# Two adaLN layers on one core: the second layer's modulation moved into the end of the latent attention

## The chip, the cores and the metric

The kernel runs on one core of a Trainium2 chip. The metric is the device time of one execution in microseconds (us); smaller is better. A core has five engines with a queue each: TensorE (PE in the profile; its weight loads are PEld), VectorE (DVE), ScalarE (ACT), GpSimd (POOL) and SyncE (SP), which here issues nearly all DMAs. They run beside each other and wait for each other through semaphores.

## The reference, cut to what matters

```python
mod = (silu(c0) @ wmod0).reshape(1, 6, 256)          # sa, ca, ga, sb, cb, gb of layer 0
ga, gb = (2*(g >= 0) - 1) * maximum(abs(g), 0.25)     # for both gates
h = layernorm(x) * (1 + ca) + sa
x = x + ga * attn0(h)     # gates[0] * latent attention + gates[1] * 16 small heads of 16
h = layernorm(x) * (1 + cb) + sb
x = x + gb * ffn0(h)      # 8 experts, dense
mod = (silu(c1) @ wmod1).reshape(1, 6, 256)          # the same six of layer 1, from c1 alone
h = layernorm(x) * (1 + ca) + sa
x = x + ga * attn1(h)     # 16 causal heads of 16 with ALiBi
h = layernorm(x) * (1 + cb) + sb
x = x + gb * ffn1(h)      # 2 shared and 16 routed experts
```

x is 1024 tokens by 256, float32; c0 and c1 are single rows of 256, so each layer's modulation is one row of 1536 numbers. Layer 1's row doesn't depend on x and isn't read before layer 1's input. The latent attention of layer 0 has 16 heads: scores of 128 + 64 features, of which 64 are turned by rotary angles, and values that come from a latent of 64 features.

## The kernel before, in words

Tokens lie in two halves of 512 (index `i`), each of four tiles of 128. Products go to PSUM: two tiles `sc` of 1024 columns, and four of 512 that are named `nn` and `mm` in turn (`mm_tile`). A float32 product stands in the profile as two MATMUL records, called passes here. The stages, in order:

1. **Start.** x arrives; 18 products of the identity with itself (L751) run on PE while nothing else can; `first_modulation` (L104) makes shift and scale of layer 0's first input out of one third of wmod0, in 8 products with one column each; `by_feature` (L213) transposes the normalised half 0; four `products` (L520) with wA follow, then half 1.
2. **The small heads of layer 0.** A first part takes 128 by 1024 scores per item (L317) and their maxima on DVE (L323). 11 such items are made ahead, and a generator `fill` (L792) puts other products between them, three parts per item: projections, `latents_by_token` (L571), `fold_weights` (L584, products L590 and L606) and last `modulation` (L115) with the five remaining thirds of both layers. For each third `rows` (L122) multiplies the repeated silu(c) with 512 columns of wmod (L126, 4 passes) and copies the result out; `rest_of` (L132) transposes parts of one row of it by products with a one (L139, one column) and forms the gates on DVE (L141 to L159). A second part, in steps, recomputes scores (L351) beside the remaining first items and multiplies with v (L383).
3. **The latent attention** (L888 on): 16 units (head pair p, half i) of 8 tiles each. `scores` (L685, maximum L689, exponential L868) runs two tiles ahead, `transposed` (L876) turns the probabilities, and a table `beside` says what else goes with which tile: in the tiles n+9 to n+12 `over_latents` multiplies a unit's probabilities with the latents in four parts of 64 products (L907, 128 passes each), after `by_latent` (L890) has transposed one over the sums, which ACT copies out as `bc` (L894); `out_part` (L925) multiplies with the folded weights. In units with i = 0 the next pair's query and key parts (L653, L668, L669) go to the tiles n+5 to n+9; `turned` (L618) has ACT scale and swap them (L628, L632) and POOL add the rotary terms (L635 to L639).
4. **The drain.** After tile 127 the last unit's four parts, `by_latent`, the transposes of half 0 (L221) and the last `out_part` are all that is left. DVE meanwhile adds half 0's residual and normalises it.
5. The experts of layer 0, then all of layer 1.

PE's order is written by hand in all stages. That of ACT, DVE and POOL is by hand up to the end of `fill`; later a planner orders them, as it does SP's. A change in `beside` thus moves ACT's and DVE's order too.

```python
def over_tiles(n, parts):
    for k in range(3):
        at(n + k, lambda: next(parts, None))
```

Of the kernel before, what the change touches and what calls it, by code (L numbers as in the profile page):

```python
# [8 lines left out]
F32 = mybir.dt.float32  # L9
# [5 lines left out]
P = 128  # L15
T = 1024
# [26 lines left out]
def adaln_two_layers(ctx: ExitStack, tc: tile.TileContext, a: dict, out: bass.AP):  # L43
# [33 lines left out]

    def modulation_third(wp, l, i):
        w = wp.tile([P, 2, 512], F32, tag="wm", name="wm")
        cols = slice(i * 512, (i + 1) * 512)  # L80
        nc.sync.dma_start(w, a[f"wmod{l}"].rearrange("(k p) m -> p k m", p=P)[:, :, cols])
        return w

# [10 lines left out]

    cs = base.tile([P, 4], F32, name="cs")
    one = base.tile([1, 1], F32, name="one")
    modT, gates_bc, by_token = {}, {}, {}
# [5 lines left out]
    def first_modulation(w):  # L103

        pm = mm_tile()
        for j in range(4):
            for k in range(2):
                nc.tensor.matmul(
                    pm[:, j : j + 1], w[:, k, j * P : (j + 1) * P], cs[:, k : k + 1], start=(k == 0), stop=(k == 1)
                )  # L110
        nc.vector.tensor_copy(modT[0][:, 0:2], pm[:, 0:2])
        nc.vector.tensor_scalar_add(modT[0][:, 2:4], pm[:, 2:4], 1.0)

    def modulation(wp, crep):


        thirds = [(0, 1), (0, 2), (1, 0), (1, 1), (1, 2)]
        wm = [modulation_third(wp, *at) for at in thirds[:3]]
        ms = {}
        yield  # L120

        def rows(n):  # L122
            l, i = thirds[n]
            ps = mm_tile()
            for k in range(2):
                nc.tensor.matmul(ps, crep[:, 2 * l + k, :], wm[n][:, k, :], start=(k == 0), stop=(k == 1))  # L126
            ms[n] = wp.tile([P, 512], F32, name="m", bufs=2)
            evacuate(ms[n], ps)
            if n + 3 < len(thirds):
                wm.append(modulation_third(wp, *thirds[n + 3]))  # L130

        def rest_of(n):  # L132
            l, i = thirds[n]
            m = ms.pop(n)
            mt = modT[l]
            pm = mm_tile()
            for j in ((0, 1, 2, 3), (6, 7), (8, 9))[i]:
# [356 lines left out]
    with pool("l0a") as l0, pool("mla") as ml:  # L494
# [198 lines left out]
        with pool("pat") as pat:  # L693
# [11 lines left out]
            with pool("absorb") as ab:  # L705
# [8 lines left out]
                with pool("first") as fp:  # L714
                    first = modulation_third(fp, 0, 0)
                    nc.sync.dma_start(wA, a["wA"].rearrange("(k p) m -> p k m", p=P))
# [31 lines left out]
                    nc.scalar.activation(cs, cT, AF.Silu)  # L748
                    ps = mm_tile()
                    for _ in range(18):  # L750
                        nc.tensor.matmul(ps[:, :P], ident, ident, start=True, stop=True)  # L751
                    norms = [normalized(i) for i in range(2)]
# [4 lines left out]
                    whole(norms[0])  # L757
                    first_modulation(first)
                    by_feature(0, 0, 0)
                    next(norms[1])  # L760
# [31 lines left out]
                def fill():  # L792
                    crep = ab.tile([P, 4, P], F32, name="crep")
                    nc.vector.tensor_copy(crep, cs.unsqueeze(2).to_broadcast([P, 4, P]))
                    with pool("wmod", 3) as wp:
                        mods = modulation(wp, crep)
                        next(mods)
                        for i in range(2):
                            project(qT, put_q, wt[1], 1, i)
                            yield  # L800
                        for t in range(NT):
                            project_v(v, wt[2], t)
                            if t % 2:
                                yield
                        yield from latents_by_token(ab)
                        yield from fold_weights(qn, wkv, wo)
                        yield from mods

# [38 lines left out]
        with pool("mla1") as m1, pool("mla2", 2) as m2:  # L847
# [47 lines left out]

            def over_latents(u, part):


                n = T // 32 // 4
                if part == 0:  # L900
                    avs[u] = [mm_tile() for _ in range(4)]
                pt, av = pts[u], avs[u]
                for b in range(n * part, n * part + n):
                    for r in range(4):
                        row = slice(32 * r, 32 * r + 32)
                        for j in range(2):
                            nc.tensor.matmul(  # L907
                                av[r][64 * j : 64 * j + 64, :P], kv32[row, b, :], pt[j][row, b, :],
                                start=(b == 0), stop=(b == 4 * n - 1),
                            )  # L910
                if part < 3:
                    return
                del pts[u], avs[u]
                cxs[u] = m2.tile([P, 4, P], F32, name="cx")
                bc = bcs.pop(u)
                for r in range(4):
                    q = slice(32 * r, 32 * r + 32)
                    nc.vector.tensor_mul(
                        cxs[u][:, :, q], av[r][:, :P].rearrange("p (t q) -> p t q", t=4), bc[:, :, q]
                    )  # L920
# [16 lines left out]

            def over_tiles(n, parts):

                for k in range(3):  # L940
                    at(n + k, lambda: next(parts, None))

            for u, (p, i) in enumerate(units):
                n = 8 * u
                if u + 1 < len(units):
                    at(n + 8, by_latent, u)
                for part in range(4):
                    at(n + 9 + part, over_latents, u, part)
                    if u + 1 == len(units) and part == 1:

                        at(n + 9 + part, by_latent, u, lambda: sc_tile()[:, :512])
                for t, m in enumerate((14, 15, 16, 16)):
                    at(n + m, out_part, u, t)
                if p + 1 < NH // 2:
                    if i == 0:
                        at(n, weights_of, p + 1)
                    over_tiles(n + 5, query_part(p + 1, i, True))
                    over_tiles(n + 6, query_part(p + 1, i, False))
                    if i == 0:
                        over_tiles(n + 6, key_part(p + 1, 0))  # L960
                        over_tiles(n + 7, key_part(p + 1, 1))
            def reload():
                for i in range(2):
                    nc.sync.dma_start(x[i], xv[:, 4 * i : 4 * i + 4, :])

            over_tiles(1, query_part(0, 1, True))
            over_tiles(3, query_part(0, 1, False))
            at(4, latents_of_odd)
            at(112, reload)
            last = 8 * len(units)  # L970
            at(last, residual, 0, gates_bc[0][:, :HID])
            at(last, lambda: whole(normalized(0)))
            at(last + 5, by_feature, 0, 1, 0, True)
            with tc.manual_schedule(engines={mybir.EngineType.PE}):
# [513 lines left out]
```

## Time and profile before

| what | us |
|---|---|
| median of 3 runs (all: 1382.57, 1378.88, 1382.86) | 1382.57 |
| the profiled execution, its own time | 1383.18 |
| its span, first to last instruction | 1381.4 |
| PE busy (share of the span) | 1322.2 (96%) |
| DVE busy | 810.2 (59%) |
| ACT busy | 605.2 (44%) |
| POOL busy | 206.7 (15%) |

The table's busy times come from the page's first part. PE is the engine with work nearly always; what counts are the places where it waits and the stretches where its clock is granted at half. Times in the text are microseconds from the span's start. In lines of the timeline the first number is the start, the second the length of the group; in brackets stands how long the engine idled before it, and what ended that. In a table of windows each engine has its busy time and the instructions that touch the window; then come the granted TensorE clock, the share of the DMA engines and GB/s.

### The profile page before, as it was taken

What the parts mean: (1) busy time and instruction counts of PE and PEld (TensorE: products, weight loads), DVE (VectorE), ACT (ScalarE), POOL (GpSimd) and SP (SyncE); (2) the same over time, 40 slices, a digit from 0 to 9 for tenths busy, and PEclk for the clock granted to TensorE, in tenths of its full rate; (3) what the DMA queues carried; (4) which work ended last, traced back from release to release, by engine and by line L of the source; (5) the groups of instructions that cost most, each with busy time, mean ns of one, the idle gap of its engine ahead of it and who ended that gap; (6) DMA issues with size and microseconds to landing.
All of it is one profiled execution on the core that took longest, in us unless ns stands there. A gap on an engine that the chain in (4) does not pass through costs nothing. (4 is left out here: it accounts for less than half of the span.)

```text
span 1381.4 us, 33034 instructions
## 1 busy us (share of the span) xinstructions
PE 1322.2 (96%) x14664; PEld 724.9 (52%) x14664; DVE 810.2 (59%) x1243; ACT 605.2 (44%) x1083; POOL 206.7 (15%) x194
## 2 busy tenths in 40 slices
PE   9999999988999999999999889999999998999998
PEld 6542323324555555555555565565556444566665
DVE  3677777735676776767676765443465766143222
ACT  4436665644655645454655322211034644511111
POOL 2000000041424334141424001000000031010000
PEclk9999999999999999999999999999999999999999
DMA  9210000000000000000001203222210000234441
GB/s 260 76 32 1 1 1 1 1 1 16 6 6 9 6 6 6 7 7 6 2 3 36 74 4 82 69 84 70 69 56 25 2 2 1 85 96 147 152 154 56
DMA packets 56600, 59.33 MB, mean 43 GB/s; under 512 B 15047, under 2 KB 42184, under 8 KB 56458
## 3 DMA queue, kind: packets, MB, share of 16 engines
q1 hardware_dynamic: 55914, 57.22, 13.8%
q8 instruction: 115, 1.88, 0.6%
q14 instruction: 27, 0.22, 0.1%
q10 hardware_dynamic: 544, 0.00, 0.0%
HBM read 55.05 MB, written 1.12 MB: 41 GB/s over the span
## 5 line engine op out<-in xcount | busy, mean ns | idle before, releaser
L323 DVE TENSOR_REDUCE mx<-sc 128x2 f32<-128x1024 f32 (+3 forms) x224 | 240.0, 1106 | 45.5 <-PE sc L317 17.3
L868 ACT ACTIVATE pr<-sc,nmax 128x1024 f32<-128x1024 f32 x128 | 142.6, 1114 | 218.8 <-DVE nmax L689 212.7
L876 DVE STREAM_TRANSPOSE pt<-pr 128x1024 f32<-128x1024 f32 x128 | 158.9, 1242 | 122.4 <-ACT pr L868 122.4
L317 PE MATMUL sc<-kT,qT 32*128 32x512 f32 (+3 forms) x896 | 211.0, 594 | 19.7 <-DVE mx L323 19.3
L351 PE MATMUL mm<-q,kT 32*128 32x512 f32 (+3 forms) x388 | 195.8, 606 | 4.5 <-DVE t L626 3.0
L351 PE MATMUL nn<-q,kT 32*128 32x512 f32 (+3 forms) x388 | 195.1, 604 | 0.5 <-DVE qf L675 0.5
L689 DVE TENSOR_REDUCE nmax<-sc 128x1 f32<-128x1024 f32 x128 | 153.9, 1203 | 16.8 <-PE sc L685 13.4
L907 PE MATMUL mm<-pt,kv 32*64 32x128 f32 x4096 | 135.2, 274 | 8.0 <-ACT bc L894 5.4
L907 PE MATMUL nn<-pt,kv 32*64 32x128 f32 x4096 | 135.4, 274 | 3.2 <-issue 1.7
L361 ACT ACTIVATE pt<-mm 128x512 f32<-128x512 f32 (+2 forms) x194 | 107.9, 556 | 60.5 <-PE nn L351 34.0
L907 PEld LDWEIGHTS mm<-pt,kv 32*64 32x64 f32 x4096 | 117.3, 130 | 32.0 <-issue 24.8
L907 PEld LDWEIGHTS nn<-pt,kv 32*64 32x64 f32 x4096 | 116.9, 130 | 28.7 <-issue 22.2
L361 ACT ACTIVATE pt<-nn 128x512 f32<-128x512 f32 (+2 forms) x194 | 107.9, 556 | 53.0 <-PE mm L351 21.4
L317 PEld LDWEIGHTS sc<-kT,qT 32*128 32x128 f32 x896 | 66.9, 186 | 116.0 <-DVE mx L323 95.8
L685 PE MATMUL sc<-kf,qf 128*128 128x512 f32 x256 | 125.7, 614 | 1.1 <-ACT pr L868 1.1
L685 PE MATMUL sc<-x,qf 128*128 128x512 f32 x256 | 123.3, 606 | 1.4 <-ACT pr L868 1.4
L635 POOL TENSOR_TENSOR t<-t,cos 128x512 f32<-128x512 f32 x32 | 41.1, 1286 | 527.4 <-ACT sw L632 268.1
L1242 DVE TENSOR_TENSOR he<-he,row 128x512 f32<-128x512 f32 x46 | 31.7, 692 | 132.9 <-ACT he L1234 107.3
L1234 ACT ACTIVATE he<-sc,b 128x512 f32<-128x512 f32 x43 | 29.6, 688 | 123.7 <-PE sc L1233 123.7
L1233 PE MATMUL sc<-hT,w 128*128 128x512 f32 x172 | 80.7, 593 | 0.0
L632 ACT COPY sw<-t 32x512 f32<-32x512 f32 x116 | 71.6, 617 | 2.0
L685 PEld LDWEIGHTS sc<-x,qf 128*128 128x128 f32 x256 | 45.5, 189 | 50.5 <-issue 46.4
(362 smaller groups left out, 2009.8 us busy)
## 6 DMA issues: line engine op xcount, KB each, us to landing
w<-in_moe_w_dram SPq DMA_DIRECT2D x50, 256.0 KB
w<-in_wg_dram SPq DMA_DIRECT2D x16, 256.0 KB
w<-in_wu_dram SPq DMA_DIRECT2D x16, 256.0 KB
w<-in_wd_dram SPq DMA_DIRECT2D x16, 256.0 KB
row<-gD SPq DMA_DIRECT2D x14, 256.0 KB
wm<-in_wmod_dram SPq DMA_DIRECT2D x6, 512.0 KB
x<-in_x_dram SPq DMA_DIRECT2D x4, 512.0 KB
wo<-in_o_dram SPq DMA_DIRECT2D x1, 2048.0 KB
```

The source lines that it names most:

```text
L317: nc.tensor.matmul(sc[:, i, :n], qT[r, g, qt * P : (qt + 1) * P], kT[r, g, c * 512 : c * 512 + n], start=True, stop=not diag,)
L323: nc.vector.tensor_reduce(mx[:, qi, c, 2 * pair : 2 * pair + 2], sc[:, :, :n], AX.X, ALU.max)
L351: nc.tensor.matmul(ps[:, q0:], kT[r, g, kc * P : (kc + 1) * P], state[u]["q2"][r, q0:], start=True, stop=not diag,)
L361: nc.scalar.activation(pt[:, 2 * pair + i, q0:], ps[:, q0:], AF.Exp)
L632: copy(sw[32 * (s ^ 1) : 32 * (s ^ 1) + 32, :], t1[32 * s : 32 * s + 32, :])
L635: nc.gpsimd.tensor_mul(t1, t1, cos[:, cols])
L685: nc.tensor.matmul(sc[:, c], qfs[p, i][j][:, t * P : (t + 1) * P], kf[p % 2][j][:, c], start=True, stop=True)
L689: nc.vector.tensor_reduce(nmax, sc, AX.X, ALU.max, negate=True)
L868: nc.scalar.activation(pr, sc, AF.Exp, bias=nmax, accum_out=sums[u][:, t, j : j + 1])
L876: nc.vector.transpose(pts[u][j][:, :, 32 * t : 32 * t + 32], prs.pop(n).rearrange("p (b k) -> p b k", k=32))
L907: nc.tensor.matmul(av[r][64 * j : 64 * j + 64, :P], kv32[row, b, :], pt[j][row, b, :], start=(b == 0), stop=(b == 4 * n - 1),)
L1233: nc.tensor.matmul(ps, w1[:, k, :], hT[i][:, k, :], start=(k == 0), stop=(k == 1))
```

## The change

- `modulation_third` loads each third into two tiles of 128 by 512 with a DMA each, instead of one tile of 128 by 2 by 512.
- Six more identity products run on PE between `first_modulation` and the first `by_feature`.
- `fill` keeps only layer 0's two thirds, and puts them ahead of `fold_weights`. Both rows are copied out by ACT now (they alternated).
- Layer 1's three thirds go to the drain: their loads are asked for in tile 116, into the buffers of the key and query parts (`sw`, `t1`); the first `rows` goes ahead of the last unit's part 0, and after each of the parts 0, 1 and 2 come the next `rows` and a `rest_of`. They use `sc` tiles.
- Of the next pair's key parts the product and first copy go one tile forward (n+5 and n+6 instead of n+6 and n+7); their second and third piece stay in their tiles. The query part that isn't turned now follows both keys' products in n+6.
- `by_feature` of half 0 is listed one tile earlier; on PE it stands after the last part, as before.

In the compiled order, 12 passes of L126 and 16 of L139 leave the stretch before the steps and stand in the drain. On DVE, layer 1's 14 gate instructions follow half 0's normalisation.

```diff
-    def modulation_third(wp, l, i):
-        w = wp.tile([P, 2, 512], F32, tag="wm", name="wm")
+    def modulation_third(l, i, tiles):
         cols = slice(i * 512, (i + 1) * 512)
-        nc.sync.dma_start(w, a[f"wmod{l}"].rearrange("(k p) m -> p k m", p=P)[:, :, cols])
-        return w
+        for k, w in enumerate(tiles):
+            nc.sync.dma_start(w, a[f"wmod{l}"][k * P : (k + 1) * P, cols])
+        return tiles
...
-        thirds = [(0, 1), (0, 2), (1, 0), (1, 1), (1, 2)]
-        wm = [modulation_third(wp, *at) for at in thirds[:3]]
+        wm = [modulation_third(*at, tiles()) for at in thirds]
...
-            ms[n] = wp.tile([P, 512], F32, name="m", bufs=2)
-            evacuate(ms[n], ps)
-            if n + 3 < len(thirds):
-                wm.append(modulation_third(wp, *thirds[n + 3]))
+            ms[n] = m_tile()
+            nc.scalar.copy(ms[n], ps)
...
                     first_modulation(first)
+                    nothing(6)
                     by_feature(0, 0, 0)
...
                         yield from latents_by_token(ab)
+                        yield from mods
                         yield from fold_weights(qn, wkv, wo)
-                        yield from mods
...
+            def over_tiles(tiles, parts):
+                for n in tiles:
+                    at(n, lambda: next(parts, None))
...
+                    for part in range(4):
+                        at(n + 9 + part, over_latents, u, part, 4)
+                        if part == 1:
+                            at(n + 9 + part, by_latent, u, lambda: sc_tile()[:, :512])
+                        for _ in range(2):
+                            at(n + 9 + part, lambda: next(mods, None))
...
-                    over_tiles(n + 5, query_part(p + 1, i, True))
-                    over_tiles(n + 6, query_part(p + 1, i, False))
+                    over_tiles((n + 5, n + 6, n + 7), query_part(p + 1, i, True))
                     if i == 0:
-                        over_tiles(n + 6, key_part(p + 1, 0))
-                        over_tiles(n + 7, key_part(p + 1, 1))
+                        over_tiles((n + 5, n + 7, n + 8), key_part(p + 1, 0))
+                        over_tiles((n + 6, n + 8, n + 9), key_part(p + 1, 1))
+                    over_tiles((n + 6,), query_part(p + 1, i, False))
...
+            mods = modulation(
+                [(1, i) for i in range(3)], lambda: [m2.tile([P, 512], F32, tag=t, name=t, bufs=3) for t in ("sw", "t1")],
+                lambda: m2.tile([P, 512], F32, name="m", bufs=2), lambda: sc_tile()[:, :512],
+            )
+            at(116, lambda: next(mods))
             last = 8 * len(units)
+            at(last, lambda: next(mods))
             at(last, residual, 0, gates_bc[0][:, :HID])
             at(last, lambda: whole(normalized(0)))
-            at(last + 5, by_feature, 0, 1, 0, True)
+            at(last + 4, by_feature, 0, 1, 0, True)
```

## The prediction, made before the change was run

> **What bounds the kernel now.** First the page: PE is busy for 96% of the span, so a gain must come from PE's waits, from half clock, or from work that moves into such waits. Next the table of windows, cut where the granted clock changes:
>
> ```profile
> 3.34:6.75 3.41, 3.41 (x18) 3.41 (x18) 1.15 (x5) 0.00 (x0) 2.40 (x5) 1.00 0.90 277
> 6.75:10.16 3.41, 2.85 (x26) 2.69 (x25) 3.09 (x13) 0.21 (x1) 1.03 (x1) 1.00 1.10 348
> 10.16:13.58 3.42, 2.77 (x14) 2.37 (x13) 1.80 (x9) 0.94 (x2) 0.95 (x1) 0.50 1.03 325
> 13.58:16.99 3.41, 3.41 (x8) 2.69 (x9) 0.49 (x2) 1.31 (x5) 0.29 (x2) 0.50 1.17 300
> ...
> 88.67:92.09 3.42, 1.85 (x11) 0.70 (x6) 3.32 (x10) 0.00 (x0) 0.00 (x0) 1.00 0.00 0
> 92.09:95.50 3.41, 3.41 (x11) 2.35 (x13) 2.58 (x3) 2.34 (x5) 0.00 (x0) 0.50 0.00 0
> ```
>
> See the clock column: it falls to half at 10.16 and at 92.09, each time for 6.83 us, on a grid of 3.41 us. Ahead of 92.09 PE was busy for 1.85 us of 3.42; ahead of 10.16 it was mostly on products of one column. Then PE's and DVE's timeline where the small heads' steps begin:
>
> ```profile
> 87.05 0.70 PE L317 MATMUL sc<-kT,qT 32*128 32x512 f32 x2 [0.55 <-DVE mx L323]
> 90.94 0.66 PE L351 MATMUL mm<-q,kT 32*128 32x512 f32 x1 [1.57 <-DVE modT L144]
> ```
> ```profile
> 85.77 2.36 DVE L323 TENSOR_REDUCE mx<-sc 128x2 f32<-128x1024 f32 x2 [0.38 <-PE sc L317]
> 88.50 1.22 DVE L323 TENSOR_REDUCE mx<-sc 128x2 f32<-128x1024 f32 x1
> 92.23 2.58 DVE L323 TENSOR_REDUCE mx<-sc 128x2 f32<-128x1024 f32 x2
> ```
>
> Between the maxima at 88.50 and 92.23 DVE forms layer 1's gates, PE stands for 1.57 us, and half clock follows. Last the waits of the latent attention and drain, and the drain in windows (PE only; x counts passes):
>
> ```profile
> PE mm L907 <- ACT bc L894: 5.4, 6, 0.9
> PE mm L907 <- issue: 2.6, 1, 2.6
> ```
> ```profile
> 812.00:813.78 1.78, 0.43 (x3) 1.00 0.00 0
> 813.78:817.87 4.09, 4.09 (x254) 1.00 0.01 4
> 817.87:819.02 1.15, 1.02 (x8) 1.00 0.00 0
> 819.02:821.10 2.08, 2.08 (x128) 1.00 0.03 8
> 821.10:822.77 1.67, 0.01 (x1) 1.00 0.00 0
> 822.77:824.84 2.07, 2.07 (x127) 1.00 0.03 8
> 824.84:827.08 2.24, 1.07 (x8) 1.00 0.00 0
> ```
>
> From 812 to 827 PE idles 1.35 us for the last probabilities, and some 3.4 us in gaps (0.56, 1.66, 1.17) that no engine's work ends. The instruction queue moved one page of 16 KB at about 816.8, 820.1 and 823.9, and each gap ends some 1.3 us after such a page: PE outruns its instructions there.
>
> **Part 1, six identities and the split load.** Twelve passes. In 3.34:6.75 a pass took some 0.21 us at the slow rate, so about 2.5 us, put ahead of the transposes at 10.86, whose inputs are ready at 10.56: nothing hides them. Below: they fill 10.16:13.58 with 2.5 us of products, full clock returns at 13.58 instead of 16.99; transposes at 13.4 take 0.9 instead of 1.95, the wait for ACT 0.66, the sixteen wA passes (0.22 each instead of 0.47) end at 18.6 instead of 18.78: -0.2. Above: the window isn't enough, transposes end at 15.1, products start at 16.0 and run at half to 20.4: they end at 21.9, +3.1. The nearest rows: a full window of identities (3.34:6.75) was followed by a faster rate, the start's partial one (1.35 to 3.34) was not; 75% lies between. I take **+1.0**. Two loads of 256 KB bring the same bytes in the same order; PE waits 0.56 us for them now, so +-0.3, taken as 0.
>
> [...]
>
> **Part 2, the stretch before the steps.** Leave: 12 passes of L126 (a third is 1.7 to 1.9 us) and 16 of L139 (0.125 each), about 7.2 us of PE; three copies (0.69) or ACT copies; layer 1's gates on DVE. What is late next is DVE: each item of L317 needs two maxima, 2.36 us. Walking the new order with these rows: both thirds 56.8 to 60.5, an item, rests to 62.5, folding. Layer 0's gates (2.9 us, as at 78.43) now push maxima back, PE idles 1.3 at 67.5 and 0.4 ahead of L333. The last three items start at 74.8, 77.7 and 80.0, with nothing put behind the last two, so DVE sets the pace: maxima at 75.9, 78.8, 81.2. The first step's maximum comes at 83.5 (88.50 now), and ten maxima at 1.23 us (99.97 on) end at 95.8, so PE reaches the first L383 at 96.9 instead of 107.23: -10.3. But in 78.44:81.85 PE would be busy 1.9 us of 3.41, as ahead of 92.09; if half clock follows, PE's 1.07 us beside each maximum becomes 2.14, and 6.83 us hold 3.2 maxima instead of 5.55: 2.9 back. **-7.4**; ends -10.3 and -5.0 (the first maximum's lead alone, 88.5 to 83.5). Nothing later gives it back: kv's and the next weights' loads are asked for here or later, and the following steps run on PE and DVE at 2.46 us each.
>
> **Part 3, key parts.** PE's pair of passes moves; the gap that it could fill is the 0.9 us in six units. There ACT is busy without a break from 407.56 to the end of bc at 423.2: query 3.1, two keys 3.1 each, the other query 1.15, exponentials. All of it still precedes bc in ACT's new order, so bc ends at 423.3. PE's scores two tiles on now wait for an exponential that ends at 421.5, and the 12 passes that ran ahead of bc come behind it: about +0.1 in seven units. **+0.7**; ends -5.4 (all gaps close) and +1.5.
>
> **Part 4, the loads.** Six DMAs of 256 KB join SP: four behind the reload of x at 750, two behind the first two expert weights, waiting for POOL's last use of their buffers (760.8), with eight weight loads queued behind. These weights are needed at 830, so that costs nothing. But PE's 2.57 us gap at 770 ends 1.4 us after an instruction page at 767.9, late because ten weight loads held the DMA engines from 759 to 767. Now 0.5 MB more runs there, but from 760.5 to 761 nothing. Ends -2.6 (the page slips through) and +4.2 (2.5 later, and a further half-clock window, 1.7); **0**, since the loads ahead of the page's request amount to about the same.
>
> [...]
>
> **Part 5, the drain.** From 812.07: rows 1.72 (in the wait that ends at 813.78), part 2.07, rows 1.72, rest 1.0, part 2.07, by_latent 0.45, 0.7 for `sc` (its last reader is DVE's shift and scale, queued behind the normalisation that ends at 821.52), rows 1.72, rest 0.5, part 2.07, rest 0.5, part 2.07, transposes 0.9: 829.6, and out_part at 829.7 instead of 827.08: **+2.6**. Parts now lie 3 to 5 us apart, so pages keep up; the stalls' 3.4 us and the wait's 1.35 hide most of 7.2. DVE's 14 instructions (4.2 us) lie at 821.5 to 827, where it idles. Ends: +1.9 (no wait for sc) and +6.0 (the gaps stay).
>
> Sum: 1.0 - 7.4 + 0.7 + 0 + 2.6 = -3.1 on 1383.18, so 1380.1; the median shown lies 0.6 below that execution, so **1379.5**.
>
> **Rivals.**
> - The clock holds: identities -0.2, no half clock after the fill, -10.3: with +0.7 and +2.6 that is -7.2, 1375.4. For: the window 313.95 to 317.36 was as empty (1.76 us) and kept its clock. Against: its products used more of the array.
> - Identities that don't do what they are for: +3.1 instead of +1.0, 1381.6. For: 75% of a window is nowhere seen to suffice. Against: of identities, 58% (1.35 to 3.34) is the most that is seen to fail.
> - Slower: instruction pages. If the drain's gaps stay beside the added products (+6.0) and the page at 770 waits for all twelve loads (+4.2), 1.0 - 7.4 + 0.7 + 10.2 = +4.5, so 1387.1. It decides from some 3.1 us of added page stalls on. For: a page took 0.9 to 1.3 us and each gap followed one. Against: gaps came after two parts back to back, and parts no longer are.
>
> **The numbers.** Forecast (1377 to 1382) 0.48; clock holds 0.27; identities 0.14; pages 0.11. A measurement can tell 0.3% from no change, 4.1 us: faster is below 1378.4, slower above 1386.7. Faster: 0.14 of the forecast and 0.24 of the first rival, 0.38. Slower: 0.08 of the last. Same: 0.54. The range, 1374 to 1385, leaves out most of the last rival and the best of the first.
>
> **What would show it.** Right: the first L383 at 95 to 100; maxima back to back from 76; no gap over 0.6 us among the drain's L907; out_part 17 to 18 us after the previous unit's; the 0.9 us waits for bc still there. Wrong: half clock to 20 us or none after 10; L907 waiting for bc no more; a stall near 765 over 3 us.

## The result, and the profile after

The changed kernel takes 1384.76 us (median of 12 runs) beside 1382.67 us for the kernel before (12 runs in turn with them): a ratio of 1.0015, 95% interval 1.0003 to 1.0027. It is about 2 us slower. The forecast was 1379.5 us, 3 us faster. The profiled execution of the changed kernel took 1387.31 us, with a span of 1385.5 us; it is 4.15 us behind that of before at the last product. Since the traces of the two kernels differ in where half clock falls, the median times rank the kernels and the traces say where.

Lines of the changed kernel are numbered a little differently (L383 is L382, L685 is L684, L907 is L912, L925 is L930), and where two numbers stand the second is its own. One after another along the trace, "later" being later than in the trace of before:

| where (PE's first instruction of the stage) | before | after | later by |
|---|---|---|---|
| second half's transposes, L221/L220 | 18.78 | 17.38 | -1.40 |
| latents' transposes in the fill | 56.19 | 56.63 | +0.44 |
| first L383/L382 | 107.23 | 102.10 | -5.13 |
| first scores of the latent attention | 320.20 | 313.81 | -6.38 |
| unit 0 over the latents, L907/L912 | 360.49 | 358.68 | -1.81 |
| unit 13 | 762.28 | 762.57 | +0.29 |
| unit 14 | 793.52 | 790.48 | -3.05 |
| the last unit's first L925/L930 | 827.08 | 827.80 | +0.72 |
| layer 1's experts, first L1233/L1251 | 1172.46 | 1176.62 | +4.15 |

Between the first scores and unit 0 the changed kernel loses 4.6 us. Some 2.5 of them are the key parts' (by no_key, below). The other 2.0 stand in no_key as well: both have a window of half clock there (321.49 to 324.90, and 319.14 to 322.55 in no_key) that the kernel before lacks. fold_first (below), with the key parts in place and no such window, takes 40.6 us for this stretch, the kernel before 40.3 and no_key 42.3.

Now the views that answer to those of before. First the table of windows of the changed kernel, with the columns as before:

```profile
10.87:14.29 3.42, 2.66 (x21) 2.05 (x19) 1.05 (x5) 1.45 (x2) 1.25 (x2) 1.00 0.99 301
14.29:17.70 3.41, 3.41 (x17) 2.96 (x18) 2.36 (x9) 1.61 (x8) 0.00 (x0) 1.00 1.21 291
...
62.08:65.49 3.41, 3.41 (x23) 2.21 (x22) 3.34 (x7) 0.00 (x0) 0.00 (x0) 1.00 0.49 103
65.49:68.90 3.41, 3.41 (x18) 3.35 (x16) 3.34 (x8) 0.60 (x1) 0.00 (x0) 0.50 0.48 102
...
72.32:75.73 3.41, 3.40 (x29) 2.69 (x25) 2.54 (x3) 0.59 (x1) 0.00 (x0) 0.50 0.00 0
82.56:85.97 3.41, 2.72 (x14) 0.60 (x8) 3.14 (x3) 0.00 (x0) 0.00 (x0) 1.00 0.00 0
85.97:89.38 3.41, 3.39 (x18) 1.17 (x16) 2.46 (x3) 0.75 (x2) 0.00 (x0) 0.50 0.00 0
```

The half clock of the start (10 to 17) is gone. But a new one of 10.24 us stands in the middle of the folding, from 65.49 to 75.73, and one window near 86 instead of two near 92. Next PE's timeline where the steps begin, then DVE's:

```profile
84.01 3.68 PE L316 MATMUL sc<-kT,qT 32*128 32x512 f32 x10 [0.69 <-DVE mx L322]
86.48 1.21 PE L350 MATMUL mm<-q,kT 32*128 32x512 f32 x1
```
```profile
82.73 4.98 DVE L322 TENSOR_REDUCE mx<-sc 128x2 f32<-128x1024 f32 x4 [0.59 <-PE sc L316]
88.59 2.57 DVE L322 TENSOR_REDUCE mx<-sc 128x2 f32<-128x1024 f32 x2 [0.88 <-PE nn L350]
```

Layer 1's gates no longer lie between the maxima, and PE's 1.57 us ahead of the first step are gone. The waits of PE in the latent attention and drain (us in total, how often, the longest):

```profile
PE sc L684 <- ACT pr L873: 13.5, 9, 2.4
...
PE nn L912 <- issue: 1.3, 2, 0.9
PE mm L930 <- DVE cx L923: 0.7, 1, 0.7
PE sc L895 <- DVE modT L143: 0.7, 1, 0.7
```

The first line decides the case (`pr` are the probabilities that the exponential writes; it has then read a tile `sc`, which comes free). The same line of the kernel before:

```profile
PE sc L685 <- ACT pr L868: 2.5, 2, 1.4
```

Before, L907 waited for bc (5.4 us in six waits) and scores for `pr` 2.5 us in two, 7.9 us in all. Now nothing waits for bc, and scores wait 13.5 us for `pr`: 5.6 us more. The wait "issue" of 2.6 us at 770 is down to 0.9. In the drain two gaps are left on PE's timeline, the predicted one for `sc` and one of 0.38 us:

```profile
818.76 0.63 PE L895 MATMUL sc<-ident,rw 128*128 128x128 f32 x4 [0.69 <-DVE modT L143]
826.48 0.32 PE L912 MATMUL nn<-pt,kv 32*64 32x128 f32 x2 [0.38 <-issue]
```

Last a unit with key parts, ACT's timeline in the changed kernel, from the exponential of tile n+7 to bc:

```profile
405.16 1.12 ACT L873 ACTIVATE pr<-sc,nmax 128x1024 f32<-128x1024 f32 x1 [3.27 <-DVE nmax L688]
...
406.27 0.59 ACT L627 ACTIVATE t<-nn 128x512 f32<-128x512 f32 x1
406.89 0.62 ACT L631 COPY sw<-t 32x512 f32<-32x512 f32 x1
407.53 0.60 ACT L627 ACTIVATE t<-mm 128x512 f32<-128x512 f32 x1
408.15 3.14 ACT L631 COPY sw<-t 32x512 f32<-32x512 f32 x5
411.32 1.12 ACT L873 ACTIVATE pr<-sc,nmax 128x1024 f32<-128x1024 f32 x1
...
415.49 2.50 ACT L631 COPY sw<-t 32x512 f32<-32x512 f32 x4
418.02 1.11 ACT L873 ACTIVATE pr<-sc,nmax 128x1024 f32<-128x1024 f32 x1
...
420.22 0.58 ACT L899 COPY bc<-nn 128x512 f32<-128x512 f32 x1
```

And PE's timeline beside it:

```profile
412.52 1.88 PE L684 MATMUL sc<-kf,qf 128*128 128x512 f32 x4
414.23 0.59 PE L930 MATMUL mm<-wvo,cx 128*128 128x256 f32 x2
414.67 1.88 PE L684 MATMUL sc<-kf,qf 128*128 128x512 f32 x4
...
417.25 0.60 PE L895 MATMUL nn<-ident,rw 128*128 128x128 f32 x4
419.28 1.98 PE L684 MATMUL sc<-kf,qf 128*128 128x512 f32 x4 [1.44 <-ACT pr L873]
```

ACT has no pause from 405.16 to 420.80: 15.64 us. The same stretch before:

```profile
407.56 1.11 ACT L868 ACTIVATE pr<-sc,nmax 128x1024 f32<-128x1024 f32 x1 [3.27 <-DVE nmax L689]
...
417.27 1.11 ACT L868 ACTIVATE pr<-sc,nmax 128x1024 f32<-128x1024 f32 x1
...
422.63 0.57 ACT L894 COPY bc<-mm 128x512 f32<-128x512 f32 x1
```

From 407.56 to 423.20 it is also 15.64 us: the same work. What differs is what lies ahead of the third exponential: it starts at 418.02, 12.9 us after the first, where before it started 9.7 us after it. PE, with both key products done early, puts two tiles' scores nearly back to back (412.52 and 414.67); both tiles `sc` are then taken, and the next scores stand until the third exponential has read one.

### The profile page after: what moved, and what is told of

The parts are those of the page before. It is cut to its first block, busy times and chain, and to the rows that moved or that the text cites. A ratio compares the mean times of both kernels' runs of the same rounds, so it can differ in the third digit from the quotient of the medians.

```text
span 1385.5 us, 33071 instructions
## 1 busy us (share of the span) xinstructions
PE 1324.4 (96%) x14676; PEld 726.6 (52%) x14676; DVE 812.2 (59%) x1240; ACT 607.1 (44%) x1086; POOL 206.2 (15%) x194
## 5 line engine op out<-in xcount | busy, mean ns | idle before, releaser
L912 PE MATMUL nn<-pt,kv 32*64 32x128 f32 x4096 | 133.6, 274 | 1.3 <-issue 1.3
L912 PE MATMUL mm<-pt,kv 32*64 32x128 f32 x4096 | 133.5, 273 | 0.0
L684 PE MATMUL sc<-x,qf 128*128 128x512 f32 x256 | 123.4, 608 | 8.1 <-ACT pr L873 8.1
L912 PEld LDWEIGHTS mm<-pt,kv 32*64 32x64 f32 x4096 | 116.8, 130 | 25.1 <-issue 20.5
L684 PE MATMUL sc<-kf,qf 128*128 128x512 f32 x256 | 124.3, 608 | 5.4 <-ACT pr L873 5.4
L912 PEld LDWEIGHTS nn<-pt,kv 32*64 32x64 f32 x4096 | 116.5, 130 | 23.3 <-issue 23.0
L1251 PE MATMUL sc<-hT,w 128*128 128x512 f32 x172 | 80.7, 593 | 0.0
L684 PEld LDWEIGHTS sc<-x,qf 128*128 128x128 f32 x256 | 45.5, 189 | 56.8 <-issue 45.1
```

Source lines behind the costliest of these rows:

```text
L684: nc.tensor.matmul(sc[:, c], qfs[p, i][j][:, t * P : (t + 1) * P], kf[p % 2][j][:, c], start=True, stop=True)
L912: nc.tensor.matmul(av[r][64 * j : 64 * j + 64, :P], kv32[row, b, :], pt[j][row, b, :], start=(b == 0), stop=(b == T // 32 - 1),)
L1251: nc.tensor.matmul(ps, w1[:, k, :], hT[i][:, k, :], start=(k == 0), stop=(k == 1))
```

## The experiments

Sixteen kernels are compared in this table, each with the kernel before on the same chip. The last column is from the traces: PE's time from the first L907/L912 of unit 0 to that of unit 13, which holds six of the seven units with key parts and neither fill nor drain. Before, it is 401.79 us.

| run | median us (before beside it) | ratio, 95% interval | unit 0 to 13, us |
|---|---|---|---|
| the changed kernel | 1384.76 (1382.67) | 1.0015, 1.0003 to 1.0027 | 403.89 |
| key_alone | 1389.11 (1383.72) | 1.0038, 1.0024 to 1.0052 | 404.46 |
| no_key | 1379.81 (1383.72) | 0.9967, 0.9956 to 0.9978 | 401.59 |
| no_ident | 1384.52 (1383.72) | 1.0005, 0.9994 to 1.0015 | 403.87 |
| in_fill | 1393.97 (1383.72) | 1.0071, 1.0053 to 1.0089 | 403.90 |
| products_only | 1382.88 (1383.40) | 1.0004, 0.9990 to 1.0017 | 403.35 |
| copies_later | 1378.31 (1383.40) | 0.9959, 0.9944 to 0.9975 | 401.61 |
| later_no_ident | 1378.37 (1383.40) | 0.9960, 0.9946 to 0.9973 | 401.61 |
| fold_first | 1382.13 (1383.40) | 0.9988, 0.9977 to 0.9999 | 401.59 |
| act_after | 1390.44 (1383.29) | 1.0052, 1.0037 to 1.0067 | 410.60 |
| act_in_place | 1380.85 (1383.29) | 0.9989, 0.9977 to 1.0000 | 402.27 |
| dve_after | 1404.47 (1383.95) | 1.0150, 1.0132 to 1.0167 | 424.21 |
| dve_in_place | 1394.46 (1383.95) | 1.0071, 1.0054 to 1.0087 | 414.70 |
| short_after | 1371.66 (1382.51) | 0.9914, 0.9900 to 0.9928 | 393.75 |
| short_in_place | 1368.99 (1382.51) | 0.9902, 0.9883 to 0.9921 | 393.73 |
| key1_later | 1369.99 (1382.51) | 0.9908, 0.9895 to 0.9920 | 394.09 |

### One part done or undone

**key_alone.** On the kernel before, `over_tiles` with a list of tiles as in the change, and

```diff
-                    over_tiles(n + 5, query_part(p + 1, i, True))
-                    over_tiles(n + 6, query_part(p + 1, i, False))
+                    over_tiles((n + 5, n + 6, n + 7), query_part(p + 1, i, True))
                     if i == 0:
-                        over_tiles(n + 6, key_part(p + 1, 0))
-                        over_tiles(n + 7, key_part(p + 1, 1))
+                        over_tiles((n + 5, n + 7, n + 8), key_part(p + 1, 0))
+                        over_tiles((n + 6, n + 8, n + 9), key_part(p + 1, 1))
+                    over_tiles((n + 6,), query_part(p + 1, i, False))
```

> The kernel before with nothing but the key parts one tile forward. Theory K (the key parts cost most of what the prediction missed): the scores two tiles on now wait for an exponential that ACT does behind the key copies, so the wait of L907 for bc (6 times 0.9 us) goes and seven waits of scores for pr take its place (about 1.4 us more each, 2.4 in the first unit). It is 3 to 6 us slower than before, and the latents of the first unit (L907) start 2 to 3 us later against the first scores. Rival D (the key parts are nearly free, as the prediction had it, and the loss lies in the drain and in half-clock windows that fell elsewhere): 0 to 1.5 us slower, no wait for pr over 1 us in the first unit.

Measured: 1.0038, so 5.3 us slower. Theory K holds and rival D falls. Unit 0 over the latents starts 43.85 us after the first scores, 3.56 us more than before; PE's timeline and the windows of this kernel say why:

```profile
355.24 3.60 PE L685 MATMUL sc<-x,qf 128*128 128x512 f32 x8
358.67 0.60 PE L890 MATMUL mm<-ident,rw 128*128 128x128 f32 x4
361.64 3.02 PE L685 MATMUL sc<-x,qf 128*128 128x512 f32 x4 [2.38 <-ACT pr L868]
```
```profile
359.03:362.45 3.42, 1.04 (x5) 0.49 (x4) 1.89 (x2) 3.35 (x7) 3.27 (x4) 1.00 0.00 0
362.45:365.86 3.41, 3.41 (x51) 1.59 (x57) 1.57 (x3) 1.46 (x3) 3.33 (x3) 0.50 0.00 0
```

The wait of 2.38 us leaves PE busy for 1.04 us of 3.42, and the next window runs at half clock, which comes on top of the wait.

**no_key.** The changed kernel with the key parts as before:

```diff
-                        over_tiles((n + 5, n + 7, n + 8), key_part(p + 1, 0))
-                        over_tiles((n + 6, n + 8, n + 9), key_part(p + 1, 1))
+                        over_tiles((n + 6, n + 7, n + 8), key_part(p + 1, 0))
+                        over_tiles((n + 7, n + 8, n + 9), key_part(p + 1, 1))
```

with the query part that isn't turned listed ahead of them again.

> The changed kernel with the key parts where they were. Theory K: 3 to 6 us faster than the changed kernel, so 1 to 4 us faster than before; the waits of scores for pr over 2 us are gone and L907 waits for bc again. Rival D: within 1.5 us of the changed kernel, 0.5 to 3 us slower than before.

Measured: 0.9967, 3.9 us faster than before by the medians and 4.6 by the ratio; against the changed kernel (0.9967 over 1.0015) 6.6 us. Waits for bc are back, and those for `pr` are as before:

```profile
PE nn L912 <- ACT bc L899: 5.2, 6, 0.9
PE sc L684 <- ACT pr L873: 2.5, 2, 1.4
```

The key parts cost 5 to 7 us, and the rest of the change is worth some 4.

**no_ident.** The changed kernel without `nothing(6)`.

> The changed kernel without the six added identity products. If the lead that they bring by 23 us is given back at the wait for qa at 33 us, as the traces suggest: within 1 us of the changed kernel, with half clock near 10 to 17 us back, by_feature of the first half earlier by 0.9 us, and PE's wait ahead of the transposes of qa near 0.8 us again. Rival (identities keep the clock for good, so the later work starts earlier): 1.5 to 3 us slower than the changed kernel. A third way: the windows of half clock at 65 to 76 us fall differently, which moves the time by up to 3 us either way.

Measured: 1.0005 beside the changed kernel's 1.0015; the intervals overlap. Half clock from 11.39 to 18.22 is back, and the lead is lost as expected: with the six identities PE reaches the second half's transposes at 17.38, without them at 18.76, and then waits for `qa` (the latents, which DVE scales) for 3.5 us in all with them and 1.9 us without. In this kernel the identities do what they are for and bring nothing: the wait behind them takes the gain.

The other traces show that it depends on the kernel. Of the thirteen kernels here that have the identities, nine kept the clock from 10 to 19 us; in_fill, act_in_place and dve_after lost it for one window and dve_in_place for two. The four without (before, key_alone, no_ident, later_no_ident) lost two each. In seven of the nine the wait for `qa` was followed by a window of half clock near 36 us (35.83 to 39.25 in no_key), which none of the four without has.

**in_fill.** The changed kernel with a second `modulation` over layer 1's three thirds in `fill`, and none in the drain:

```diff
                         yield from mods
+                        next(mods1)
                         yield from fold_weights(qn, wkv, wo)
+                        yield from mods1
```

> The changed kernel with layer 1's three thirds back behind the folding, and no modulation in the drain; identities, key parts and layer 0's thirds as changed. If the move to the drain pays as predicted in sign (fill shorter by some 5 us, drain longer by some 4, the gap at 770 shorter): 0 to 4 us slower than the changed kernel, with the first L383 3 to 6 us later and the last out_part following the previous unit's some 4 us sooner. Rival D (the drain costs more than the fill gains): 1 to 4 us faster than the changed kernel.

Measured: 1.0071, 7.7 us slower than the changed kernel: the sign as expected, the size nearly twice the upper end. The first L382 comes at 112.37, 10.3 us later, with half clock at 96.42 to 103.25 once more; that is more than the 3 to 6 us of the expectation, and the drain gives back only 2.4 us (unit 14 to the last L930: 34.94 us instead of 37.32). Rival D falls: against this kernel the move to the drain pays. How much of the 7.7 us is the move's stays open. In key_alone too all five thirds lie in the fill, all behind the folding, and it is at 1.0038, 4.6 us below in_fill.

**fold_first.** no_key with the two thirds of layer 0 behind `fold_weights` again (`yield from mods` moved back).

> The changed kernel with the key parts in place, and layer 0's two thirds behind the folding again, as before. By the prediction's walk the order matters little, since the gain is layer 1's work that left: within 2 us of the version with the key parts in place, first L383 at 98 to 102 us. Rival: layer 0's gates on DVE lie between the first maxima again and set off half clock, so the first L383 comes 3 us later or more and the time is 2 to 4 us longer.

Measured: 0.9988, about 2.9 us slower than no_key (0.9967). The rival is nearly right: layer 0's gates lie between the maxima on DVE, and the windows of this kernel show DVE full, PE nearly empty, and three windows at half clock.

```profile
80.13:83.54 3.41, 0.62 (x4) 0.50 (x4) 3.34 (x8) 0.00 (x0) 0.00 (x0) 0.50 0.00 0
83.54:86.95 3.41, 3.22 (x12) 1.02 (x12) 2.36 (x3) 0.00 (x0) 0.00 (x0) 0.50 0.00 0
86.95:90.37 3.42, 3.42 (x20) 1.18 (x16) 1.88 (x3) 1.19 (x3) 0.00 (x0) 0.50 0.00 0
```

The first of the three is the empty window itself; in the one ahead of it PE is busy for 2.87 us of 3.42. The first L382 comes at 102.39, 2.65 us after that of no_key, where the rival had said 3 or more.

### Why the key parts cost so much

**products_only** and **copies_later.** Two edits of no_key that were to part TensorE's half of the move from ACT's. The first puts a `yield` between the key products and `turned` and lists the parts with n+5 and n+6 as first tile; the second delays copies:

```diff
-                        over_tiles((n + 7, n + 8, n + 9), key_part(p + 1, 1))
+                        over_tiles((n + 7, n + 9, n + 10), key_part(p + 1, 1))
```

> The changed kernel with only TensorE's half of the key parts' move: both key products stand one tile forward, but ACT reads them out and copies them where it did before. Theory A (the loss comes from ACT's order: two key halves are copied between two exponentials, so no exponential ends for some 7 us, and the scores behind wait for their bank): within 1 us of the version with the key parts in place, which was 3.9 us faster than the kernel before, and no wait of scores for pr over 1.5 us. Rival P (the place of the products on PE is what costs, since they keep banks and the scores' turn): most of the 6 us between that version and the changed kernel is back, so 0 to 3 us slower than the kernel before.

> The changed kernel with the key parts in place, and the four copies of the second key half one tile later each instead of earlier, behind bc on ACT. Theory A: bc ends 1.25 us sooner in six units, so its 0.9 us wait (5.2 us in all) goes and nothing on ACT is late in its place: 4 to 5.5 us faster than the version with the key parts in place, 8 to 10 us faster than the kernel before. Rival: another wait of about the same length stands behind bc (for the reciprocal sums or for the exponential of the tile after), and it gains less than 2 us.

Both failed as experiments. ACT's order is the planner's, not the program's: in products_only ACT took the key halves out in the same tiles as in the changed kernel (waits for `pr` 12.6 us), in copies_later it copied where no_key does (waits for bc 5.3 us, 401.61 us from unit 0 to 13). So products_only repeats the changed kernel's loss, and copies_later is a second run of no_key, 0.9959 beside 0.9967. Neither says which half of the move costs.

**later_no_ident.** copies_later without the six identities.

> The same, copies one tile later, without the six added identity products. If the lead of 1.4 us that they bring is lost at the wait for qa: within 1 us of the version with them, half clock near 10 to 17 us is back. Rival: 1.5 to 3 us slower than with them.

Measured: 0.9960 beside 0.9959. The identities are worth nothing here too.

**act_after** and **act_in_place.** ACT follows the program's order in the latent attention, on the changed kernel and on no_key:

```diff
-            with tc.manual_schedule(engines={mybir.EngineType.PE}):
+            with tc.manual_schedule(engines={mybir.EngineType.PE, mybir.EngineType.Activation}):
```

> The changed kernel, key parts forward as changed, but in the latent attention ACT too runs in the order in which the program gives its work, as TensorE does already: the exponential of each tile, then the copies of that tile, instead of copies gathered ahead of the exponentials. Theory A (the scheduler's order on ACT is what makes the moved key parts dear, not their place on TensorE): scores' waits for pr (13.5 us in all) fall below 4 us and L907's wait for bc does not come back, so it is 6 to 13 us faster than the changed kernel, 4 to 11 us faster than the kernel before. Rival P (the place of the products costs): the scores still wait 8 us or more in all. Rival W: ACT now waits for maxima at the head of its order with copies behind it, and TensorE waits for the copies instead: no faster than the changed kernel.

> The same order written out for ACT, with the key parts in their old place. Theory A: bc's waits (5.2 us) and scores' waits (2.5 us) fall below 2 us in all, so it is 3 to 7 us faster than the version with the key parts in place (7 to 11 us faster than the kernel before), and it differs by less than 2 us from the one with the key parts forward. Rival P: 4 us or more faster than the one with the key parts forward. Rival W: slower than the version with the key parts in place and ACT's order left to the scheduler.

Theory A in this form fell: act_after is slower than the changed kernel (1.0052 beside 1.0015), act_in_place some 3 us slower than no_key (0.9989 beside 0.9967). ACT's timeline of act_after:

```profile
412.51 1.11 ACT L873 ACTIVATE pr<-sc,nmax 128x1024 f32<-128x1024 f32 x1 [2.38 <-DVE nmax L688]
...
418.03 1.11 ACT L873 ACTIVATE pr<-sc,nmax 128x1024 f32<-128x1024 f32 x1 [1.50 <-DVE nmax L688]
...
422.90 0.57 ACT L899 COPY bc<-nn 128x512 f32<-128x512 f32 x1
```

That is rival W: the key products push the scores and so the maxima back, ACT stands idle for 3.88 us with copies ready behind the exponentials, and L912 waits for bc (9.3 us in seven waits). The planner's order, which fills that time with copies, was the better one. What remained was the sum itself.

**dve_after** and **dve_in_place.** The eight copies of 32x512 of a key pair on DVE:

```diff
-                copy = nc.vector.tensor_copy if early else nc.scalar.copy
+                copy = nc.vector.tensor_copy if early or on_dve else nc.scalar.copy
```

> The changed kernel, key parts forward as changed, with the eight 32x512 copies of each pair of key halves on DVE (0.42 us each there by the trace of before) instead of ACT (0.62 each). Theory S (in the units with key parts ACT has some 15.6 us of work without a break from one exponential to bc, more than TensorE has; a product put ahead of the scores then only makes maxima and exponentials later): with 4.9 us taken from that chain it is ACT no more that sets the pace, the scores' waits for pr fall from 13.5 to below 4 us and L912 does not wait for bc: 6 to 12 us faster than the changed kernel, 4 to 10 us faster than the kernel before. Rival V: DVE, with maxima and transposes behind the copies, becomes the one that is late, and the waits stay at 8 us or more in all under another name.

> The same eight copies on DVE, with the key parts in their old place. Theory S: bc's waits (5.2 us) go, so it is 3 to 6 us faster than the version with the key parts in place, 7 to 10 us faster than the kernel before, and within 2 us of the one with the key parts forward. Rival V: no faster than the version with the key parts in place, with DVE named in TensorE's waits.

Rival V, with a price that nobody had named: 1.0150 and 1.0071. In dve_after the waits for `pr` grew to 25.5 us; in dve_in_place L912 waits 8.9 us in six for a sum on DVE (L931). DVE's timeline of dve_after, and POOL's:

```profile
417.05 4.64 DVE L631 COPY sw<-t 32x512 f32<-32x512 f32 x4
421.73 1.23 DVE L688 TENSOR_REDUCE nmax<-sc 128x1 f32<-128x1024 f32 x1
```
```profile
415.89 2.71 POOL L635 TENSOR_TENSOR sw<-sw,sin 128x512 f32<-128x512 f32 x2
418.56 2.85 POOL L638 TENSOR_TENSOR qf<-t,sw 64x512 f32<-64x512 f32 x2
```

Four copies that take 0.42 us each elsewhere took 4.64 us while POOL ran its rotary products, and the maximum stood behind them. The experiment says nothing for or against theory S.

**short_after** and **short_in_place.** To take work from ACT and give it to nobody, one copy of 128x512 replaces the four copies of each key half; the keys' halves are not swapped, so part of the computation is left out:

```diff
+            if short and not early:
+                nc.scalar.copy(sw, t1)
+                yield
-            for s in range(4):
+            for s in range(0 if short and not early else 4):
```

> The changed kernel, key parts forward, but one copy of 128x512 (0.59 us) in place of the four copies of 32x512 (2.5 us) of each key half, so the halves of the keys are not swapped: part of the computation is left out. Nothing is given to another engine. Theory S (what is late is ACT's sum of work: two key halves, a query half and the exponentials before the next exponential that frees a score bank): 3.8 us less for ACT in each of seven units, so the scores' waits for pr (13.5 us in all) fall below 3 us, no wait for bc takes their place, and it is 6 to 12 us faster than the changed kernel, at or below the version with the key parts in place. Rival P (the products' place on TensorE costs by itself): the scores' waits stay at 8 us or more.

> The same one copy instead of four in each key half (part of the computation left out), with the key parts in their old place. Theory S: bc's waits (5.2 us) go too, 4 to 8 us faster than the version with the key parts in place, and within 1.5 us of the run with the key parts forward and the short copies: then the move by itself costs nothing. Rival P: 4 us or more faster than that run.

Measured: 0.9914 and 0.9902. With key parts forward the waits for `pr` fall from 13.5 us to 2.9 us:

```profile
PE sc L687 <- ACT pr L876: 2.9, 3, 1.4
```

From unit 0 to 13 the two take 393.75 and 393.73 us: the place of the key products makes no difference once ACT has 3.8 us less to do. By the runs they lie 1.7 us apart, with intervals that overlap. Rival P falls; theory S holds, though both gains are larger than it said: 14.0 us on the changed kernel for 6 to 12, and 9.0 on no_key for 4 to 8.

**key1_later.** The whole work, and the second key half in the other direction:

```diff
-                        over_tiles((n + 7, n + 8, n + 9), key_part(p + 1, 1))
+                        over_tiles((n + 8, n + 9, n + 10), key_part(p + 1, 1))
```

on no_key.

> The changed kernel with the first key half in its old place and the second one tile later than before (the other direction than the change). By theory S's sums, from the exponential of tile 7 ACT has 11 us to do before the exponential of tile 9 is out, while TensorE has 13.9 us up to the scores that need its bank; and bc no longer has the second half's 3.1 us ahead of it: the waits of L912 for bc (5.2 us) go and none of scores for pr over 0.5 us comes, so 3 to 6 us faster than the version with the key parts in place, 7 to 10 us faster than the kernel before. Rival P, or a bank that is freed late (the second half's product now takes one ahead of the four of L912): within 2 us of the version with the key parts in place, or slower.

Measured: 0.9908, 0.9895 to 0.9920: 12.5 us faster than the kernel before, and the fastest kernel here that does the whole computation. ACT's timeline of key1_later:

```profile
400.16 1.11 ACT L873 ACTIVATE pr<-sc,nmax 128x1024 f32<-128x1024 f32 x1 [3.27 <-DVE nmax L688]
...
409.85 1.12 ACT L873 ACTIVATE pr<-sc,nmax 128x1024 f32<-128x1024 f32 x1
...
412.23 0.57 ACT L899 COPY bc<-mm 128x512 f32<-128x512 f32 x1
412.94 0.60 ACT L627 ACTIVATE t<-nn 128x512 f32<-128x512 f32 x1
```

and PE's:

```profile
412.68 1.88 PE L684 MATMUL sc<-kf,qf 128*128 128x512 f32 x4
414.49 0.33 PE L912 MATMUL mm<-pt,kv 32*64 32x128 f32 x2
```

bc ends 12.64 us after the first exponential's start instead of 15.64; the second half's 3.1 us come behind it, where ACT had idled. Neither scores nor L912 wait in these units. The gain from unit 0 to 13 is 7.5 us, 1.25 us for each of the six. By the ratios the kernel is 8.2 us faster than no_key (0.9908 over 0.9967), so this stretch holds nearly all of it. That is more than the 3 to 6 us expected, which went by the 5.2 us of waits for bc. The wait's row understates its cost: in no_key unit 2's first part over the latents takes 5.15 us, 1.2 more than the 3.94 of the others, of which the row names 0.9.

## Why the prediction was wrong, step by step

- **Part 3, the key parts: the step that failed.** It said that the scores two tiles on wait for an exponential, and that this costs "about +0.1 in seven units", +0.7 with an upper end of +1.5. It costs 4.8 us in the traces (2.5 from the first scores to unit 0 and 2.3 from unit 0 to 13, the changed kernel against no_key) and 5.3 to 6.6 us by the runs. The mechanism was seen: that exponential was forecast to end at 421.5, 13.9 us after the first one's start, and it ends 14.0 us after (419.13 less 405.16). The price of the wait was wrong, in two terms. In the six later units it is 0.38 us (after against no_key) to 0.45 us (key_alone against before) each: PE loses 1.7 us ahead of L912 and gets back 1.2 us behind it, as bc is no longer waited for. In unit 0 the new wait is 2.4 us. The waits for bc were six, the units with key parts seven: in unit 0 there was no wait for bc that could be given back. Why the wait itself is longer there (2.4 us for 1.4) was not tried. In key_alone a window of half clock came on top. The text also said that the 0.9 us waits for bc would still be there; they went.
- **Part 1, identities.** +1.0 was put down, within -0.2 and +3.1. In this kernel's trace they keep the clock up to 17.7 us as the better case said, and bring 1.4 us; in four other kernels they don't keep it. But the sum ended at 22 us; it took no account of the wait for `qa` further on, which is 1.6 us longer than in no_ident. By two pairs of runs they are worth nothing, within about 2 us.
- **Part 2, the fill.** -7.4, first L383 forecast at 96.9 and with half clock 99.8. From 56 us to the first L382 the changed kernel gained 5.57 us (-5.13 less +0.44), between the two ends. No_key, products_only and copies_later run the same fill and reach it at 99.74, 99.41 and 100.43, 7.5, 7.8 and 6.8 us ahead of before; they have no half clock in the folding, while the changed kernel's trace has 10.24 us of it. So the size was right and half clock near 84 us was foreseen; the other one, in the folding, wasn't. The size is in part luck. Two windows of half clock were counted and there is one, and the maxima were to stand back to back from 76: in no_key, without half clock in the folding, DVE still idles 2.72 us ahead of those at 77.40. That layer 0's thirds ahead of the folding matter (2.9 us, fold_first) was no term of the sum: the walk had them in the new place and did not price the old.
- **Part 4, loads and the gap at 770.** 0 was taken, with ends -2.6 and +4.2. The gap went from 2.57 to 0.94 us, and the half clock behind it (771.34 to 774.75 before) is gone: 3.3 us from unit 13 to unit 14. Why the gap shrank was not tried by itself, but two runs bear on it: key_alone and in_fill, without the loads in tile 116, stand 1.95 and 2.09 us at this place, while no kernel with the loads stands more than 1.6 us there. The half clock is another matter: key_alone and in_fill have none there either.
- **Part 5, the drain.** +2.6; it is 3.8 us by the trace (from unit 14 to the last unit's first L930, 33.56 to 37.32). The predicted wait for `sc` is there, with 0.69 us for 0.7, and one gap of 0.38 us is left of 3.4 us. What was short is the sum of the pieces: rows took 1.8 to 1.9 us for 1.72, part 0 took 2.4 us for 2.07, and the gap of 0.38 us was not in it.
- **The rivals.** None of the three was the case. The clock did not hold, the identities did not fail in the changed kernel, and the gaps put down to instruction pages shrank (2.57 to 0.94 us at 770, some 3.4 to 0.38 us in the drain). The slower side came from a term that the sum held at 0.7. The prediction's own signs said so: L907 waits for bc no more, the first L382 (102.10) is outside 95 to 100, and the last unit's first L930 comes 19.8 us after the previous unit's first (827.80 less 807.99), not 17 to 18.
- **What stays open.** After 827 the two profiled executions drift apart by another 3.4 us, about 2.6 of it at windows of half clock that fall elsewhere (1045.11 to 1048.52 and 1161.16 to 1167.99, where the kernel before has 1160.46 to 1163.87 alone). Nothing of the change is in that stretch; a profile shows one fall of these windows, and the 12 runs of the changed kernel spread from 1378.61 to 1388.36 us.

Without Part 3 the terms come to -3.8 us; no_key, which is the change without it, measured -3.9 us. That agreement is luck. In no_key's trace Part 2 is -7.5, but the identities bring nothing, the stretch with the gap at 770 is 3.2 us shorter where 0 was taken, the drain is 4.0 us longer for 2.6, and 2.0 us go ahead of unit 0, where a window of half clock stands that no term held.

## What to carry to other kernels

When a step is moved on the engine that is the bound, add up the work of the engine behind it from one fixed point to the next (here ACT, 15.6 us from an exponential to bc, with a third exponential in it that frees a PSUM tile), and compare it with what the first engine does in the same stretch: here moving TensorE's products forward only made room that TensorE had to wait in, and moving a key half behind bc instead took 3 us out of that chain. A wait that goes from one name to another ("bc" to "pr") is not a gain; sum the waits of all names, count how many units have the wait that is to be traded in, and measure a stage from start to start too, since a wait's row can understate its cost (0.9 for 1.2 us here). Where a planner orders the other engines, an edit of the program's order may hardly reach them: look at the order that came out before anything is concluded from the time.

## What the runs showed of the hardware

DVE's copies and POOL's products were slower beside each other. In dve_after a copy of 32x512 from SBUF to SBUF on DVE has a median of 0.42 us and a longest of 1.40 us. Four of them took 4.64 us in a row at 417.05, while POOL ran its two-operand products of 1.3 us each; three of them at 411.99, where POOL had been idle for over 20 us, took 1.28 us. POOL's own products took 1.34 us for 1.27 and 1.39 us for 1.27, dve_after against the kernel before. That one slows the other, and by what means, was not shown: no run here had the same copies with POOL idle in the same place.

The granted clock fell to half after a window in which PE was busy for 1.04 us of 3.42 (key_alone), but also after one in which it was busy all through, with single-column products, products of 64 columns and 1.84 us of scores (62.08 to 65.49 in the changed kernel). Of the thirteen kernels with this fill (in_fill and fold_first have another), five had that half clock and eight kept full clock. Where the 3.41 us grid lies does not explain it by itself. The window ends 2.74 us after the first folding product in the changed kernel (65.48 less 62.74). In no_key, reckoned back on the grid from the change at 83.62, it ends 2.78 us after it (66.55 less 63.77) and holds the same products; there the clock stayed. A busy PE was no assurance here; what decides was not tried.
